# Layer 1's attention rewritten: 32x32 turns on VectorE, value products in four row strips, division on GpSimd

## The chip, the core and the metric

The program runs on one core of a Trainium2 chip. TensorE (PE, with its weight loads shown as PEld) multiplies, VectorE (DVE), ScalarE (ACT) and GpSimd (POOL) do the rest, SyncE (SP) issues most of the DMAs. SBUF and PSUM have 128 partitions[...]. All data is fp32. The metric is the device time of one execution in microseconds.

## The reference

Two layers on x of 8 x 256 x 128 (8 batches of 256 tokens, width 128). Each layer is `x + attention(layernorm(x)) + ffn(layernorm(x))`. Layer 0 has attention with 16 heads of 8 and eight experts of which each token uses two, besides a shared expert. Layer 1, cut to what matters:

```python
q = (x @ Wq + bq)            # 8 heads of 128 a token
k, v = split(x @ Wkv + bkv)  # one key head and one value head of 128
q, k = q + pe, k + pe
scores = (q @ k.T) / sqrt(128)            # causal, inside each batch of 256 tokens
attn = softmax(scores) @ v
out = attn.reshape(2048, 1024) @ Wo
# ffn: one of 8 experts a token (router: softmax, argmax)
h = gelu(x @ w1[e] + b1[e])               # 128 -> 512
y = (h @ w2[e] + b2[e]) * score           # 512 -> 128
```

## The kernel before

The residual stream `acc` stays in SBUF as 16 tiles of 128 tokens; `xT` is the normalised input, turned, with the width on the partitions. Layer 0 fills the first 364 us of the trace: its scores are made in 32-row strips of PE (L768 and L814, two strips each), its experts' tokens come by gathers on POOL (`take`, L464, an indirect DMA for 128 rows), and a small plan (`at_place`) says between which score groups the experts, the way back and layer 1's first layer norms and projections are written. It changes in nothing but what is said under the change.

Layer 1 starts at L1060 with the last of four layer norms, the values (`l1_values`), the router and `routing`, which sorts the tokens into 24 tiles of 128, each with one expert; it is a generator that is moved on a piece at a time. `l1_project` makes q and k of a block of two batches, nine products of 512 columns, each taken out of PSUM by DVE with bias and position added (L701).

The attention of a batch has four steps, by group of four heads (`hg`) and half of the queries (`t`). For t = 0 only 128 keys count, for t = 1 all 256. `l1_probs` multiplies scores into a two-bank PSUM tile, adds the causal mask on DVE (L1090), takes the row maximum (L1092), scales it (L1094), makes four exponentials on ACT with their sums (L1098), and divides on DVE head by head (L1109). `l1_pv`, called for the step before, turns the weights by PE (L1118, a product with the identity for each 128x128 block), copies them out of PSUM on DVE (L1120) and ACT (L1122), multiplies with v (L1125, 512 columns at a time, one PSUM bank tagged `held`), and copies the result to `oT` on ACT (L1128). After the fourth step `l1_finish` multiplies with Wo (L1136) and adds to `acc` (L1144).

Between batches 3 and 4 stand the 24 expert tiles (`l1_group`, six groups of four): a gather of the group's tokens (L466), a turn by PE, four products with w1 (L1039), four Gelus on ACT (L1048), four products with w2 (L1025), bias on DVE (L1032), result to HBM. The weights of a tile (256 + 256 + 64 KB) go through a ring of five, loaded by SP as a tile is done with. Then sixteen gathers fetch every token's result (L1165), and batches 6 and 7 add them to `acc` (L1184).

Nothing here sets an order by hand: the framework schedules the instructions of each engine from the program's order and its own estimates. PSUM is two tiles of two banks for scores (`big`), three single banks (`bank`) and one more (`held`).

Of the kernel before, what the change touches and what calls it, by code (L numbers as in the profile page):

```python
# [10 lines left out]
F32 = mybir.dt.float32  # L11
# [5 lines left out]
P = 128  # L17
# [11 lines left out]
NE = 8  # L29
# [31 lines left out]
def two_layer_kernel(  # L61
# [47 lines left out]

    def ctile(shape, name, pool=const):  # L110
        return pool.tile(shape, F32, tag=name, name=name)
# [82 lines left out]
    pe_s = ctile([P, S], "pe_s")  # L194
    b1_s = ctile([P, NE, NFT], "b1_s")
# [24 lines left out]

    dram = ctx.enter_context(tc.tile_pool(name="dram", bufs=1, space=bass.MemoryType.DRAM))
    xd = [dram.tile([NT, E], F32, name=f"xd{n}") for n in range(2)]
    yg = [dram.tile([n * P, E], F32, name=f"yg{i}") for i, n in enumerate((NS0, NS1))]
# [56 lines left out]
    def layernorm(layer, blk):  # L280
# [4 lines left out]
        for t in range(TPB):  # L285
            nc.vector.bn_stats(st[:, t, :], acc[:, blk * TPB + t, :])
            nc.vector.bn_aggr(mv[:, t, :], st[:, t, :])
        rs = small.tile([P, TPB], F32, tag="ln_rs", name=f"rs_{nm}")
        nc.gpsimd.tensor_scalar_add(rs, mv[:, :, 1], EPS_LN)
        nc.gpsimd.tensor_tensor(rs, rs, minus_half, ALU.pow)  # L290
        off = small.tile([P, TPB], F32, tag="ln_off", name=f"off_{nm}")
        nc.vector.scalar_tensor_tensor(off, mv[:, :, 0], -1.0, rs, ALU.mult, ALU.mult)
        xn = work.tile([P, TPB, E], F32, tag="xn", name=f"xn_{nm}")
        ps = bank(f"lnT_{nm}")
        for t in range(TPB):
            nc.scalar.activation(
                xn[:, t, :],
                acc[:, blk * TPB + t, :],
                AF.Identity,
                bias=off[:, t : t + 1],  # L300
                scale=rs[:, t : t + 1],
            )
            nc.tensor.transpose(ps[:, ts(t, P)], xn[:, t, :], ident)
        nc.scalar.copy(xT[:, ts(blk, BLK)], ps)
# [4 lines left out]
    def softmax8(lg, nm, n):  # L309

        m = small.tile([P, n], F32, tag="r_m", name=f"r_m_{nm}")
        nc.vector.tensor_reduce(m, lg, AX.X, ALU.max)
        d = small.tile([P, n, NE], F32, tag="r_d", name=f"r_d_{nm}", bufs=2)
        nc.vector.tensor_tensor(d, lg, m.unsqueeze(2).to_broadcast([P, n, NE]), ALU.subtract)
        nc.scalar.activation(d, d, AF.Exp)
        s = small.tile([P, n], F32, tag="r_s", name=f"r_s_{nm}")
        nc.vector.tensor_reduce(s, d, AX.X, ALU.add)
        r = small.tile([P, n], F32, tag="r_r", name=f"r_r_{nm}")
        nc.vector.reciprocal(r, s)
        sc = small.tile([P, n, NE], F32, tag="r_sc", name=f"r_sc_{nm}", bufs=2)  # L320
        nc.vector.tensor_tensor(sc, d, r.unsqueeze(2).to_broadcast([P, n, NE]), ALU.mult)
        return sc

    def first_max(sc, nm, n):

        m = small.tile([P, n], F32, tag="f_m", name=f"f_m_{nm}")
        nc.vector.tensor_reduce(m, sc, AX.X, ALU.max)
        key = small.tile([P, n, NE], F32, tag="f_key", name=f"f_key_{nm}", bufs=2)
        nc.vector.tensor_tensor(key, sc, m.unsqueeze(2).to_broadcast([P, n, NE]), ALU.is_equal)
        nc.vector.tensor_tensor(key, key, rev.unsqueeze(1).to_broadcast([P, n, NE]), ALU.mult)  # L330
        k = small.tile([P, n], F32, tag="f_k", name=f"f_k_{nm}")
        nc.vector.tensor_reduce(k, key, AX.X, ALU.max)
        oh = small.tile([P, n, NE], F32, tag="f_oh", name=f"f_oh_{nm}", bufs=2)
        nc.vector.tensor_tensor(oh, key, k.unsqueeze(2).to_broadcast([P, n, NE]), ALU.is_equal)
# [6 lines left out]
    def routing(nm, ohs, n, r):  # L341
# [8 lines left out]
        if len(ohs) > 1:  # L350
            sel = st([P, NTILE, NE], "sel")
            nc.vector.tensor_tensor(sel, ohs[0], ohs[1], ALU.add)
        flat = sel.rearrange("p t e -> p (t e)")
        ps = bank(f"rank_{nm}")
        nc.tensor.matmul(ps[:, :N], lhsT=tri, rhs=flat, start=True, stop=True)
        nc.tensor.matmul(ps[:, ds(N, N)], lhsT=ones, rhs=flat, start=True, stop=True)
        slot = st([P, NTILE, NE], "slot")
        nc.vector.tensor_copy(slot.rearrange("p t e -> p (t e)"), ps[:, :N])
        tot = st([P, NE, NTILE], "tot")
        nc.vector.tensor_copy(tot, ps[:, ds(N, N)].rearrange("p (t e) -> p e t", e=NE))  # L360
        yield
        upto = st([P, NE, NTILE], "upto")
        nc.vector.tensor_tensor_scan(
# [6 lines left out]
        )  # L370
        more = st([P, NE, NTILE], "more")
        nc.vector.tensor_tensor(
# [4 lines left out]
        )  # L377
        yield
        nc.vector.tensor_tensor(tot, upto, tot, ALU.subtract)
        nt = st([P, NE], "nt")  # L380
        nc.vector.tensor_reduce(nt, more, AX.X, ALU.add)
        end = st([P, NE], "end")
        nc.vector.tensor_tensor_scan(end, ones[:, :NE], nt, 0.0, ALU.mult, ALU.add)
        first = st([P, NE], "first")
        nc.vector.tensor_tensor(first, end, nt, ALU.subtract)
        yield
        nc.vector.tensor_tensor(slot, slot, tot.rearrange("p e t -> p t e"), ALU.add)
        nc.vector.scalar_tensor_tensor(
# [6 lines left out]
        )  # L395
        yield
        past = st([P, n, NE], "past")
        nc.vector.tensor_tensor(
# [4 lines left out]
        )  # L403
        r.expert = st([P, n], "ef")
        nc.vector.tensor_reduce(r.expert, past, AX.X, ALU.add)
        nc.vector.tensor_scalar_min(r.expert, r.expert, float(NE - 1))
        r.expert_i = st([P, n], "ei", I32)
        nc.vector.tensor_copy(r.expert_i, r.expert)
# [5 lines left out]
        for k, oh in enumerate(ohs):  # L414
            at = st([P, NTILE, NE], "at")
            nc.vector.tensor_tensor(at, slot, oh, ALU.mult)
            pf = st([P, NTILE], "pf")
            nc.vector.tensor_reduce(pf, at, AX.X, ALU.add)
            pos = st([P, NTILE], f"pos{k}", I32)
            nc.vector.tensor_copy(pos, pf)  # L420
# [3 lines left out]
            nc.vector.tensor_scalar(cut[:, 0, :], pos, 7, None, ALU.arith_shift_right)  # L424
            nc.vector.tensor_scalar(cut[:, 1, :], pos, P - 1, None, ALU.bitwise_and)
            part = st([P, 2, NTILE], "part")
            nc.vector.tensor_copy(part, cut)
            yield
            for q in range(0, NTILE, 4):
                row = work.tile([P, 4, P], F32, tag="ys", name=f"row_{nm}_{k}_{q}")  # L430
                nc.vector.tensor_tensor(
                    row,
                    lane.unsqueeze(1).to_broadcast([P, 4, P]),
                    part[:, 1, ds(q, 4)].unsqueeze(2).to_broadcast([P, 4, P]),
                    ALU.is_equal,
                )
# [312 lines left out]
    for n in range(H1 + 1):  # L749
        at_place(PROJECT1 + n, lambda: next(project1, None))  # L750
# [528 lines left out]
```

## Time and profile before

| what | value |
|---|---|
| runs | 624.95, 628.90, 629.09 us; median 628.9 |
| profiled execution | 657.19 us, span of the trace 655.4 us |
| mean granted clock of TensorE | 0.922 |
| layer 0, 0 to 364 us | PE busy 300.6, DVE 225.8, ACT 131.4, POOL 98.2 us |
| layer 1, 364 to 655.4 us | PE busy 242.2, DVE 167.5, ACT 128.0, POOL 41.5 us |
| end of the output products of batches 0, 1, 2 | 401, 431, 455 us |
| first and last expert product | 479.1 and 543.4 us |
| end of the output products of batches 4, 5, 6, 7 | 577, 604, 628, 652 us |

The trace is of one execution, which took longer than the runs without the profiler. "Busy" is the time in which an engine had an instruction at work; PE's matmuls overlap, so its busy time is more than it needs at full rate. A wait is named by the engine and line that ended it.

### The profile page before, as it was taken

How to read it: one execution, taken by the hardware profiler on the slowest of the kernel's cores; microseconds unless marked ns; L12 is line 12 of the kernel's file. 1: busy time of each engine (PE TensorE's matmuls, PEld its weight loads, DVE VectorE, ACT ScalarE, POOL GpSimd, SP SyncE). 2: the span in 40 equal slices, each digit the busy share in tenths (PEclk: the TensorE clock that was granted, in tenths of full speed). 3: DMA queues.
4: the chain of work that ended last, by engine and by line, in shares of the span. 5: the costliest groups of instructions: out<-in, count | busy, mean ns of one | idle time of the engine just before them, and what ended most of it. 6: DMA issues, size and time to landing. Idle time of an engine off the chain costs nothing.

```text
span 655.4 us, 10882 instructions
## 1 busy us (share of the span) xinstructions
PE 542.7 (83%) x3766; PEld 377.1 (58%) x3766; DVE 393.3 (60%) x961; ACT 259.4 (40%) x686; POOL 139.7 (21%) x177
## 2 busy tenths in 40 slices
PE   2879958989888898768899778989898887689786
PEld 2445636566665674525435556676487786366564
DVE  3688934556667665375685598866762423266753
ACT  0732213354445442131333533243568744132532
POOL 8500052222222204553100000004033204400000
PEclk9985988999999999598799979999898999799889
DMA  8200413234343401110100006001038992100000
GB/s 203 64 3 20 132 33 102 75 99 132 105 112 87 68 18 46 36 49 22 28 17 1 18 0 166 16 1 32 1 112 259 194 264 65 53 9 1 9 9 9
DMA packets 53383, 43.70 MB, mean 67 GB/s; under 512 B 5200, under 2 KB 48272, under 8 KB 53328
## 3 DMA queue, kind: packets, MB, share of 16 engines
q1 hardware_dynamic: 48704, 35.09, 19.1%
q0 software_dynamic: 4048, 7.65, 5.7%
q8 instruction: 30, 0.49, 0.3%
q10 hardware_dynamic: 576, 0.27, 0.2%
q14 instruction: 25, 0.20, 0.1%
HBM read 35.64 MB, written 7.34 MB: 66 GB/s over the span
## 4 chain that ended last, share of the span: by engine, by line
PE 60%; DVE 12%; ACT 11%; issue 7%; POOL 5%; another core or an unknown queue 4%; DMA 1%; SPq 0%; POOLq 0%; ACTq 0%; DVEq 0%
PE s L768 8%; PE o L1125 5%; PE s L1082 5%; PE u L600 5%; PE pv L841 5%; PE wo L1136 4%; PE qk L694 4%; PE s L814 4%; PE d L617 4%; ACT p L1098 3%; PE pT L1118 3%; DVE mx L783 3%; PE qk L512 2%; PE u L1039 2%
## 5 line engine op out<-in xcount | busy, mean ns | idle before, releaser
L466 POOL DMA_INDIRECT xs<-xd,d_ids_l x64 | 64.3, 1004 | 271.5 <-DVE d_ids_l L462 123.8
L826 ACT ACTIVATE eT<-s 128x1024 f32<-128x1024 f32 x64 | 65.3, 1024 | 133.2 <-PE s L814 101.0
L768 PE MATMUL s<-qk 32*128 32x256 f32 x512 | 85.8, 437 | 23.8 <-DVE mx L783 19.1
L783 DVE TENSOR_REDUCE mx<-s 128x4 f32<-128x1024 f32 x64 | 77.5, 1217 | 19.7 <-remote 9.1
L814 PE MATMUL s<-qa,qk 32*128 32x256 f32 x512 | 79.4, 429 | 1.1 <-DVE qa L795 0.7
L768 PEld LDWEIGHTS s<-qk 32*128 32x128 f32 x512 | 48.1, 200 | 50.2 <-DVE mx L783 26.9
L1082 PE MATMUL s<-kT,qT 128*128 128x128 f32 (+1 forms) x256 | 55.7, 355 | 16.8 <-ACT p L1098 16.8
L466 POOL DMA_INDIRECT yt<-yg,d_pos_l x48 | 48.3, 1006 | 90.7 <-DMA yg<-ys 58.7
L1125 PE MATMUL o<-pT,v 128*128 128x512 f32 x96 | 52.8, 662 | 10.9 <-ACT oT L1128 7.2
L1082 PEld LDWEIGHTS s<-kT,qT 128*128 128x128 f32 x256 | 41.3, 203 | 29.8 <-ACT p L1098 23.5
L1098 ACT ACTIVATE p<-s,ms 128x128 f32<-128x128 f32 (+1 forms) x128 | 52.2, 426 | 13.4 <-DVE ms L1094 10.4
L814 PEld LDWEIGHTS s<-qa,qk 32*128 32x128 f32 x512 | 47.1, 199 | 12.3 <-issue 5.6
L1128 ACT COPY oT<-o 128x512 f32<-128x512 f32 x32 | 18.9, 589 | 81.6 <-PE o L1125 71.2
L841 PE MATMUL pv<-eT,va 128*32 128x256 f32 x512 | 43.4, 409 | 1.2 <-ACT eT L826 1.2
L600 PE MATMUL u<-xg,gu_s 128*88 128x128 f32 x320 | 43.0, 278 | 0.6 <-ACT qk L519 0.6
L585 DVE SCALAR_TENSOR_TENSOR sg<-sg,u 88x256 f32<-88x256 f32 x40 | 16.6, 416 | 43.2 <-ACT sg L584 33.2
L617 PE MATMUL d<-dn_s,h 88*128 88x128 f32 x160 | 29.3, 306 | 12.4 <-issue 8.1
L600 PEld LDWEIGHTS u<-xg,gu_s 128*88 128x88 f32 x320 | 38.1, 161 | 1.9 <-ACT qk L519 1.5
L617 PEld LDWEIGHTS d<-dn_s,h 88*128 88x128 f32 x160 | 22.1, 199 | 26.2 <-issue 20.1
L1136 PEld LDWEIGHTS wo<-wo_s,oT 128*128 128x128 f32 x256 | 32.5, 201 | 5.9 <-issue 5.9
L1048 ACT ACTIVATE h<-u,own_b 128x128 f32<-128x128 f32 x96 | 26.6, 378 | 20.6 <-PE u L1039 20.6
L1090 DVE TENSOR_TENSOR s<-s,mask 128x512 f32<-128x512 f32 x32 | 22.2, 694 | 19.7 <-PE s L1082 10.4
(221 smaller groups left out, 937.2 us busy)
## 6 DMA issues: line engine op xcount, KB each, us to landing
w_up<-in_w_dram SPq DMA_DIRECT2D x30, 256.0 KB
gu_s<-in_gu_dram SPq DMA_DIRECT2D x40, 176.0 KB
w_down<-in_w_dram SPq DMA_DIRECT2D x18, 256.0 KB
yg<-ys SPq DMA_DIRECT2D x16, 256.0 KB
dn_s<-in_dn_dram SPq DMA_DIRECT2D x40, 88.0 KB
xd<-xn SPq DMA_DIRECT2D x8, 256.0 KB
bias<-in_b_dram SPq DMA_DIRECT2D x24, 64.0 KB
acc<-in_x_dram SPq DMA_DIRECT2D x4, 256.0 KB
```

The source lines that it names most:

```text
L466: nc.gpsimd.indirect_dma_start(out=dst, out_offset=None, in_=table, in_offset=bass.IndirectOffsetOnAxis(ap=index, axis=0), bounds_check=ta ...
L600: nc.tensor.matmul(ps[:IC, ts(c, P)], lhsT=gu0_s[:, i % RING0, c, :], rhs=xg0.get(i), start=True, stop=True,)
L617: nc.tensor.matmul(ps[:, :P], lhsT=h0[i][:, c, :], rhs=dn0_s[:, i % RING0, c, :], start=(c == 0), stop=(c == 1),)
L768: nc.tensor.matmul(pv[:, jj, t, :], lhsT=qT[r : r + ROW, g, ds(o + t * P, P)], rhs=kT[r : r + ROW, g, ds(o, S)], start=True, stop=True,)
L783: nc.vector.tensor_reduce(m[:, ds(2 * half, 2), :, D0 * ((g + 1) % NG)], pv, AX.X, ALU.max, negate=True)
L814: nc.tensor.matmul(pv[:, jj, c, :], lhsT=kT[r : r + ROW, g, ds(o + c * P, P)], rhs=qa[r : r + ROW, g, :], start=True, stop=True,)
L826: nc.scalar.activation(eT.rearrange("p j c q -> p (j c q)"), ps, AF.Exp, scale=SC0)
L841: nc.tensor.matmul(po[ds(ROW * j, ROW), ts(g % 2, S)], lhsT=va_flat[:, ds(o, ROW)], rhs=eTs[j // 2][:, j % 2, c, :], start=(c == 0), stop= ...
L1082: nc.tensor.matmul(sc[:, hh, :], lhsT=qT[:, 4 * hg + hh, ds(o + t * P, P)], rhs=kT[:, ds(o, nk)], start=True, stop=True,)
L1098: nc.scalar.activation(p[:, hh, :], sc[:, hh, :], AF.Exp, bias=ms[:, hh : hh + 1], scale=SC1, accum_out=sums[:, hh : hh + 1],)
L1125: nc.tensor.matmul(po, lhsT=v1[:, 2 * b + c, :], rhs=pT[:, c, :], start=(c == 0), stop=(c == t))
L1136: nc.tensor.matmul(ps[:, ts(t, P)], lhsT=oT[:, h, ts(t, P)], rhs=wo1_s[:, h, :], start=(h == 0), stop=(h == H1 - 1),)
```

## The change

The diff wraps nearly every instruction of the kernel in `seq(...)`, which from layer 1 on (`ordered[0] = True`) asks the scheduler to keep the order of the program; in layer 0 it does nothing. Beyond that:

- The factor 1/sqrt(128) goes into Wq, its bias and a copy of the positions (`l1_scale`, three operations on POOL), so that the maximum needs no scaling.
- A batch has three parts of 128 x 1024 weights instead of four steps: all heads of t = 0, and two halves of the heads of t = 1.
- The division is one operation a part on POOL (the last part of the last batch on DVE).
- The weights are turned by DVE in 32x32 blocks (`l1_turn`), SBUF to SBUF, without PE. Partition strip n (32 rows) then holds, for every block of 32 keys, the weights of the queries of strip n.
- So v is needed on every strip: `l1_values` writes it to HBM (`vd`), and `l1_spread` reads it back four times, once for each strip, a batch ahead, two buffers.
- `l1_pv` multiplies in four 32-row strips, each into a PSUM bank of its own, over blocks of 32 keys up to the diagonal; it runs one batch late. Four copies (`l1_out`) bring the banks to `oT`.
- Layer norm, values, router, routing, projections, gathers and the adding of results are written into fixed places of the parts (`at1`, `fill`). The last projections are spread over two batches. Fetching the experts' results is written as two gathers a place.
- The expert tiles are written with the first product of a tile before the second of the one before it, in one block, with all exponentials before or after it.
- The end is split: the output of the last batch is made for each half of the queries.

In `routing` a matmul is written one piece after the operations that make its inputs. The diff without the wrapping, cut:

```diff
+    ordered = [False]
+    def seq(ins):
+        return tc.keep_in_program_order(ins) if ordered[0] else ins
...
+    def l1_scale():
+        for dst, src in ((wq1_s, wq1_s), (bq1_s, bq1_s), (peq_s, pe_s)):
+            nc.gpsimd.tensor_scalar_mul(dst, src, SC1)
...
+    at_place(TILES + 10, l1_scale)
...
-    v1 = const.tile([P, NTILE, P], F32, tag="va", name="v1")
+    NQ1 = P // ROW
+    NK1 = S // ROW
+    vrep = const.tile([P, 2, NK1, P], F32, tag="va", name="vrep")
...
+    def l1_spread(b):
+        for n in range(NQ1):
+            nc.sync.dma_start(
+                vrep[ds(ROW * n, ROW), b % 2],
+                vd[ds(b * S, S), :].rearrange("(j k) c -> k j c", k=ROW),
+            )
...
+    def l1_experts():
+        l1_gathered(0)
+        for i in range(NS1 + 1):
+            if i < NS1:
+                l1_up(i)
+            if i % GRP == GRP - 2 and i // GRP + 1 < NS1 // GRP:
+                l1_gathered(i // GRP + 1)
+            if i > 0:
+                l1_down(i - 1)
...
+    PARTS = ((0, 0, H1), (1, 0, H1 // 2), (1, H1 // 2, H1 // 2))
...
-        for hh in range(4):
-            nc.vector.tensor_scalar_mul(p[:, hh, :], p[:, hh, :], rec[:, hh : hh + 1])
+    def l1_weigh(u):
+        rec = small.tile([P, H1], F32, tag="rec1", name=f"rec1_{u.name}")
+        seq(nc.vector.reciprocal(rec[:, : u.nh], u.sums[:, : u.nh]))
+        engine = nc.vector if u.b + 1 == B and u.h0 > 0 else nc.gpsimd
+        seq(engine.tensor_tensor(
+            u.p, u.p, rec[:, : u.nh].unsqueeze(2).to_broadcast([P, u.nh, u.nk]), ALU.mult
+        ))
...
-            for hh in range(4):
-                nc.tensor.transpose(ps[:, ts(hh, P)], p[:, hh, ts(c, P)], ident)
-            if c == 0:
-                nc.vector.tensor_copy(pT[:, c, :], ps)
-            else:
-                nc.scalar.copy(pT[:, c, :], ps)
+    def l1_turn(u):
...
+        seq(nc.vector.transpose(
+            turned[u.b, u.t][:, ds(u.h0, u.nh), :].rearrange("p h k -> p (h k)"),
+            u.p.rearrange("p h k -> p (h k)"),
+        ))
+    def l1_banks(b):
+        return [bank(f"o_{b}_{n}") for n in range(NQ1 - 1)] + [held(f"o_{b}")]
+    def l1_pv(b, t, po):
+        pT = turned[b, t].rearrange("p h (j q) -> p h j q", q=ROW)
+        for j in range(NQ1 * (t + 1)):
+            for n in range(NQ1):
+                end = NQ1 * t + n
+                if j <= end:
+                    r = ROW * n
+                    seq(nc.tensor.matmul(
+                        po[n][:, ts(t, H1 * ROW)],
+                        lhsT=vrep[r : r + ROW, b % 2, j, :],
+                        rhs=pT[r : r + ROW, :, j, :],
+                        start=(j == 0),
+                        stop=(j == end),
+                    ))
...
+    def l1_previous(b):
+        nonlocal oT
+        if b > 0:
+            po = l1_banks(b - 1)
+            for t in range(2):
+                l1_pv(b - 1, t, po)
+            if b + 1 < B:
+                l1_spread(b + 1)
+            oT = work.tile([P, H1, S], F32, tag="c", name=f"oT_{b - 1}")
+            l1_out(slice(None), po, oT)
     for b in range(B):
+        u = [Part(b, k) for k in range(len(PARTS))]
...
+        l1_scores(u[0])
+        if late is not None:
+            l1_turn(late)
+        l1_maxima(u[0])
+        l1_scores(u[1])
+        l1_maxima(u[1])
+        l1_exp(u[0])
+        l1_previous(b)
+        l1_weigh(u[0])
+        fill(b, 0)
         if b == B // 2:
+            l1_exp(u[1])
+            l1_weigh(u[1])
+            l1_turn(u[0])
+            l1_finish(b - 1, (0, 1), oT)
+            l1_experts()
+        l1_scores(u[2])
+        l1_maxima(u[2])
+        if b != B // 2:
+            l1_exp(u[1])
+            l1_turn(u[0])
+        for _ in range(2):
+            next(project1, None)
+        if b != B // 2:
+            l1_weigh(u[1])
+        fill(b, 1)
+        for _ in range(3 - b % 2):
+            next(project1, None)
+        l1_exp(u[2])
...
+        l1_weigh(u[2])
+        l1_turn(u[1])
+        if b > 0 and b != B // 2:
+            l1_finish(b - 1, (0, 1), oT)
+        fill(b, 2)
+        late = u[2]
```

## The prediction

> **What bounds the kernel now.** I read the page's chain of waits first, for where the end is decided. Shares of the span by engine:
>
> ```profile
> PE 60%; DVE 12%; ACT 11%; issue 7%; POOL 5%; another core or an unknown queue 4%; DMA 1%; SPq 0%; POOLq 0%; ACTq 0%; DVEq 0%
> ```
>
> TensorE holds most of it, yet the chain changes engine all the time, so none is full. Then I cut layer 1, which alone is rewritten, into stages by the dates of the output products (L1136), and asked for the busy time of each engine in each. Columns: stage in us, its length, busy us (instructions) of PE, weight loads, DVE, ACT, POOL; granted clock, DMA share, GB/s.
>
> ```profile
> 402.00:432.00 30.00, 27.31 (x131) 18.73 (x130) 21.74 (x50) 10.07 (x38) 0.00 (x0) 0.94 0.26 64
> 432.00:456.00 24.00, 21.17 (x126) 16.36 (x126) 15.67 (x43) 9.93 (x38) 8.15 (x8) 1.00 0.08 20
> 456.00:478.00 22.00, 18.72 (x68) 11.05 (x67) 17.05 (x37) 8.70 (x29) 0.00 (x0) 0.92 0.01 3
> 478.00:544.00 66.00, 58.04 (x450) 54.17 (x449) 23.19 (x62) 47.23 (x132) 16.02 (x16) 0.97 0.78 207
> 551.00:571.00 20.00, 10.64 (x35) 6.17 (x36) 6.83 (x21) 3.70 (x11) 12.71 (x13) 0.83 0.27 72
> 577.00:604.50 27.50, 24.80 (x118) 16.23 (x117) 20.96 (x48) 9.97 (x38) 0.00 (x0) 1.00 0.02 5
> 604.50:628.00 23.50, 20.10 (x105) 15.13 (x105) 15.09 (x39) 9.98 (x38) 0.00 (x0) 0.93 0.02 7
> 628.00:655.40 27.40, 19.02 (x89) 13.46 (x87) 12.53 (x30) 8.57 (x30) 0.00 (x0) 0.88 0.04 10
> ```
>
> Three things are to be seen. A batch without projections takes 23.5 us although PE, which overlaps its own records, needs far less: its full-speed pitch in the timeline is 0.11 us a record of 128 columns (26 records of L1136 in 3.06 us), so scores 5.1, products 5.1, output 3.4 and transposes 2.6 make 16.3 us. The rest is latency between engines. Second, the experts (478 to 544) are held by DMA after a slow start; 3-us stages of the same view, the first two before and the others after it filled:
>
> ```profile
> 479.00:482.00 3.00, 3.00 (x22) 2.84 (x22) 1.50 (x3) 1.77 (x8) 2.29 (x3) 1.00 0.36 96
> 482.00:485.00 3.00, 3.00 (x27) 2.97 (x26) 2.20 (x4) 2.95 (x6) 1.00 (x1) 1.00 0.25 79
> 524.00:527.00 3.00, 2.22 (x20) 1.98 (x20) 1.28 (x3) 0.56 (x3) 0.00 (x0) 1.00 0.91 282
> 527.00:530.00 3.00, 3.00 (x30) 3.00 (x28) 0.29 (x1) 2.18 (x8) 0.00 (x0) 1.00 0.93 271
> ```
>
> From 491 to 539 the mean is 242 GB/s at a share of 0.9 to 1.0. Third, in 551 to 571 sixteen gathers follow each other on POOL, and ACT and DVE stand with no releaser on record:
>
> ```profile
> ACT oT L1128 <- remote: 10.5, 2, 6.5
> PEld o L1125 <- ACT oT L1128: 7.0, 2, 4.8
> DVE pT L1120 <- remote: 5.9, 2, 5.0
> ```
>
> In the chain these "unknown queue" steps are 14.8 us here and 13.0 us at 88 and 269 us, both also bursts of gathers.
>
> **What the Trainium skill says.** *GPSIMD Engine Reference*, 3.1: a two-input tensor_tensor of 2048 fp32 takes 4497 ns. The trace has 1273 ns for 512 (POOL, L896), 2.5 against 2.2 ns an element; they agree roughly. Its section 8 says that GpSimd shares SBUF interfaces with VectorE; no row shows what that costs. *TensorEngine Tiling (Array Packing)*, Key Properties: 32-row tiles load and multiply in parallel, and Gotcha 1 wants different PSUM banks. The trace agrees: sixteen records (8 matmuls of 256 columns, two a strip) need 1.16 us where one matmul takes 0.43:
>
> ```profile
> 355.03 1.16 PE L814 MATMUL s<-qa,qk 32*128 32x256 f32 x16
> ```
>
> *ScalarE: Activation LUTs*, What ACT_TABLE_LOAD costs: 1283 ns for a change of set; the trace has exactly 1283, seven times each at L1048 and L1098.
>
> **The change part by part**, per batch.
> (1) PE. Removed: 24 transposes, 2.6 us. The 6 products of 512 columns (5.1 us) become 36 of 256 columns in strips. Strip 3 has 12 in a row, 12 x 0.43 + 0.2 = 5.4 us (bounds: 5.1, and 15.4 if strips never overlapped). Scores, projections and output stay.
> (2) DVE. Removed: four pT copies of 0.68, 2.7; sixteen divisions, (19.0 + 14.4)/8 = 4.2; four scalings of the maximum, 0.7. Added: three 32x32 turns of 1024. L855 takes 0.71 for 512 and L867 0.44 for 256, so 1.25 each (bounds 1.2 to 1.4), 3.75. Masks and maxima stay within 0.4. DVE falls by some 4 us.
> (3) ACT. pT copies go (1.2); sixteen exponentials and four copies stay. About 8.8 us, beside other work.
> (4) POOL. Three products of 128x1024 by the reciprocal. From L896, 1273/512 x 1024, less one fixed part, 2.45 us; the page's rate gives 2.25. I take 2.4; bounds 2.2 and, if it shares ports badly, 5.
> (5) DMA. Values go to HBM and return fourfold, 512 KB a batch, a batch ahead: at 200 GB/s 2.6 us, hidden behind a batch of 17 us. On SP a spread waits for the strip products that still read its buffer. Behind the spread of batch 2 stand the first five weight tiles (15 DMAs, issued from 396.5 us before, now after batch 1's routing, some 420; used at 485), behind that of batch 5 the sixth tile's, whose own buffer comes free later still, and behind those of batches 6 and 7 output stores that nobody waits for. Nothing charged.
> (6) Start. A scaling of wq1 (POOL, 128x1024, one input, about 1.0) comes ahead of the first layer-norm power at 15.4 us, on which ACT's first xn waits: +1 us. Its load has landed by 16 us, when the DMA rate falls to 26 GB/s. Bounds 0 and 3. The rest of layer 0 is reordered a little; 0 +/- 2, since PE bounds it as before.
> (7) Order. In the built queue of POOL the gathers are not where the source has them: eight (groups 0 and 1) stand ahead of the third product of batch 3, and after the experts ten stand ahead of batch 4's third product, then six ahead of batch 5's first. A gather costs 1.0 + 0.3 us.
>
> **The path of a batch.** From the turn of the last part (0): turn 1.25, strip products from 1.4 to 6.9 on PE, scores of part 3 to 8.6, mask and maximum to 10.6, turn 11.8, reciprocal 12.0, POOL product of part 2 to 14.6, of part 3 to 17.0, next turn. So **17.1 us without projections** against 23.5. Projections put 2 x 0.7 before the reciprocal: 18.6; routing fills DVE, so batches 1 and 2 take 20.4 and 21. Batch 3: product 2 ends at 16.0, eight gathers to 26.4, product 3 to 28.8: 28.9 (PE idle 10 us). Batch 5: 18.6 + 0.8 behind six gathers + 2 for a cold PE clock (0.5 at 497 us) = 21; batch 6 with its combine 17.5.
> Batch 0 with the layer norm now behind POOL's first product, values and router: 363 to 399, before 402.
> Experts: start at batch 4's turn + 15.5. PE alone would need 24 x 1.8 = 43 us, but nineteen tiles of 576 KB, the gathers and the results are 13.5 MB, 56 us at 242 GB/s, and the last tile. Fourteen table loads become two, 15 us of ACT, but what this buys is the slow start alone: 479 to 491 at a mean of 137 GB/s, (242 - 137) x 12 / 242 = 5.2 us. So 59 for the 64.3 between the first and the last expert product (479.1 to 543.4).
> After the experts: result lands 3.4 (543.4 to 546.8 before), ten gathers 13, product 2.4: 19 until the turn. Tail of batch 7, with one product on DVE and the last output split in two: 29.5.
>
> | from | before | after |
> |---|---|---|
> | batch 0 | 39 | 36 |
> | batches 1, 2, 3 | 30, 24, 22 | 20.4, 21, 28.9 |
> | batch 4 with experts | 99 | 15.5 + 59 + 19 = 93.5 |
> | batches 5, 6, 7 | 27.5, 23.5, 27.4 | 21, 17.5, 29.5 |
> | sum | 292.4 | 267.8 |
>
> That is -24.6 of the span of 655.4 (execution 657.2): 632.6. The median of the runs is 628.9, 0.957 of the profiled execution. At that scale the gain is 23.5 us: 605. Whether the stalls of 14.8 us exist in runs without the profiler I can't see; the 28 us between profile and median equal all such stalls. Some of the gain may thus not be there, so I take **608**.
>
> **Rivals.**
> A. *The experts lose their DMA limit*: with ACT out of the way weights stream evenly at the 339 GB/s of one 3-us stage, and PE's 43 us plus fill is the bound, 48. For it: PE at full pitch in 527 to 530. Against: the share of 0.9 to 1.0. 59 - 48 = 11 less: 595.
> B. *The stalls are the profiler's*, or return under the new bursts: 14.8 x 0.957 = 14 us less gain, 620. For it: the 28 us. Against: they sit only on bursts of gathers.
> C. *GpSimd becomes the bound, slower.* About 17 products lie on the path (two a batch, three in batch 0). At 2.4 + 1.45 us each the gain is gone; from 4.3 us the kernel is over 1% slower. At 5 us, DVE and POOL shutting each other out: 17 x 2.6 - 24.6 = +20, 648. For it: shared interfaces. Against: the new DVE work reads one SBUF input.
> D. *The strips don't overlap while they accumulate*: 10 us a batch, 685. Against: the L814 row.
> That the change doesn't do what it says is partly true already: the gathers leave the written order; charged above.
>
> **Chances**: forecast 0.52 (600 to 614), A 0.20, B 0.18, C 0.07, D 0.03. Within 1% (6.3 us, what can be told from none here) is half of B and the edge of C, slower the rest of C and D: faster 0.80, same 0.11, slower 0.09. The range takes in A with POOL at 2.2 and B: 580 to 626.
>
> **What will show it.** Right: groups of 36 strip products near 5.4 us; POOL 128x1024 near 2.4 us; unprojected batch near 17 us; experts near 59 us at a DMA share above 0.9; PE idle 10 us or more before the last turns of batches 3 and 4. Wrong: POOL beyond 4 us; strip products beyond 7; experts under 52, or a batch of 20 and more.

## The result, and the profile after

| | runs | median us | range us | profiled execution us |
|---|---|---|---|---|
| before | 20 | 627.24 | 620.91 to 635.34 | 657.19 (span 655.4) |
| after | 20 | 632.16 | 627.47 to 641.63 | 631.16 (span 629.4) |

After takes 1.0092 of before, 95% interval 1.0064 to 1.0119: 0.9% slower, where 608 us were forecast. Ratios and their intervals leave out runs over 1.5% above the fastest of their kernel; medians and ranges are of all runs.

Yet the profiled executions say the opposite, 26 us less, and after's span of 629.4 is close to the 631 that the forecast's sum gives. That agreement is luck: 10.8 of the 26 us lie in layer 0 (its last addition to `acc` is at 369.5 us in before, at 358.7 in after), where the forecast had no gain at all. The work was to find which of the two, profile or runs, was not what it seemed.

On some occasions of measurement every kernel, before included, took 25 to 40 us longer, and its profile then had engines waiting for an unknown releaser; the first profile of before is of that kind, its timed runs are not. So a time below is given with that of before on the same occasion.

The chain of waits of after, shares of the span by engine; the "unknown queue" of before is gone:

```profile
PE 49%; DVE 21%; issue 7%; POOL 7%; DMA 7%; ACT 5%; SPq 2%; ACTq 0%; POOLq 0%; DVEq 0%
```

Layer 1 of after, cut at its first scores, then at the turn (L1179) of each batch's last part, and at the end. Columns as before: stage in us, its length, busy us of PE, weight loads, DVE, ACT and POOL, granted clock, DMA share, GB/s.

```profile
358.40:392.69 34.29, 24.30 (x124) 18.75 (x122) 20.95 (x53) 9.21 (x38) 6.92 (x5) 0.82 0.29 70
392.69:414.77 22.08, 19.07 (x136) 15.06 (x139) 18.26 (x33) 8.61 (x36) 5.71 (x3) 0.92 0.09 25
414.77:440.15 25.38, 19.06 (x137) 14.20 (x133) 21.08 (x36) 8.61 (x36) 5.68 (x3) 0.93 0.49 139
440.15:470.81 30.66, 26.90 (x204) 21.39 (x202) 21.45 (x33) 8.78 (x36) 14.14 (x11) 0.93 0.14 35
470.81:561.51 90.70, 72.92 (x554) 65.81 (x554) 25.05 (x48) 38.52 (x134) 31.73 (x29) 0.91 0.59 167
561.51:581.80 20.29, 17.73 (x118) 13.78 (x119) 16.04 (x22) 8.62 (x36) 11.75 (x9) 0.82 0.18 46
581.80:598.57 16.77, 16.77 (x158) 14.73 (x158) 15.48 (x20) 8.61 (x36) 5.69 (x3) 1.00 0.18 48
598.57:629.40 30.83, 24.10 (x208) 20.45 (x202) 18.25 (x24) 11.59 (x44) 3.79 (x2) 0.89 0.09 26
```

Against the prediction's column (36, 20.4, 21, 28.9, 93.5, 21, 17.5, 29.5) only batch 2, the third row, is off by more than 3 us. The sum is 271.0 us for 267.8. Layer 1 of after came out as worked out; the gain was lost ahead of it, and in the layer 1 of before that it was measured against.

### The profile page after: what moved, and what is told of

Same layout as the page of the kernel before. It is cut to its first block, busy times and chain, and to the rows that moved or that the text cites. A ratio compares the mean times of both kernels' runs of the same rounds, so it can differ in the third digit from the quotient of the medians.

```text
span 629.4 us, 11372 instructions
## 1 busy us (share of the span) xinstructions
PE 522.2 (83%) x4054; PEld 378.2 (60%) x4054; DVE 382.5 (61%) x771; ACT 233.9 (37%) x662; POOL 187.5 (30%) x203
## 4 chain that ended last, share of the span: by engine, by line
PE 49%; DVE 21%; issue 7%; POOL 7%; DMA 7%; ACT 5%; SPq 2%; ACTq 0%; POOLq 0%; DVEq 0%
PE s L788 8%; PE u L619 5%; PE pv L861 4%; PE d L636 3%; POOL yt L485 3%; PE o L1196 3%; PE s L834 3%; PE s L1134 3%; DVE pT L1179 3%; DMA w_up<-in_w_dram 3%; DVE mx L803 3%; PE wo L1215 2%; PE u L1065 2%; ACT p L1154 2%; PE d L1083 2%
## 5 line engine op out<-in xcount | busy, mean ns | idle before, releaser
L846 ACT ACTIVATE eT<-s 128x1024 f32<-128x1024 f32 x64 | 65.3, 1024 | 117.5 <-PE s L834 117.5
L788 PE MATMUL s<-qk 32*128 32x256 f32 x512 | 88.4, 448 | 15.4 <-DVE mx L803 11.3
L1154 ACT ACTIVATE p<-s,m 128x256 f32<-128x256 f32 (+1 forms) x128 | 52.5, 441 | 108.8 <-DVE m L1148 89.1
L1166 POOL TENSOR_TENSOR p<-p,rec 128x1024 f32<-128x1024 f32 x23 | 43.9, 1910 | 147.8 <-DVE rec L1164 120.5
L834 PE MATMUL s<-qa,qk 32*128 32x256 f32 x512 | 81.6, 439 | 1.0 <-DVE qa L815 0.7
L788 PEld LDWEIGHTS s<-qk 32*128 32x128 f32 x512 | 49.6, 205 | 42.1 <-DVE mx L803 19.8
L1196 PE MATMUL o<-pT,vrep 32*128 32x256 f32 x576 | 52.5, 438 | 13.8 <-DVE pT L1179 12.8
L1196 PEld LDWEIGHTS o<-pT,vrep 32*128 32x128 f32 x576 | 41.7, 215 | 23.5 <-DVE pT L1179 14.7
L1134 PE MATMUL s<-kT,qT 128*128 128x128 f32 (+1 forms) x256 | 49.9, 352 | 3.3 <-ACT p L1154 3.3
L1215 PE MATMUL wo<-wo_s,oT 128*128 128x128 f32 x256 | 34.6, 300 | 5.2 <-DVE qT L720 2.8
L1179 DVE STREAM_TRANSPOSE pT<-p 128x1024 f32<-128x1024 f32 x24 | 29.5, 1228 | 15.5 <-POOL p L1166 15.5
L713 PE MATMUL qk<-xT,wq_s 128*128 128x512 f32 x64 | 33.2, 633 | 6.1 <-DVE qT L720 3.8
```

Source lines behind the costliest of these rows:

```text
L788: seq(nc.tensor.matmul(pv[:, jj, t, :], lhsT=qT[r : r + ROW, g, ds(o + t * P, P)], rhs=kT[r : r + ROW, g, ds(o, S)], start=True, stop=True,))
L834: seq(nc.tensor.matmul(pv[:, jj, c, :], lhsT=kT[r : r + ROW, g, ds(o + c * P, P)], rhs=qa[r : r + ROW, g, :], start=True, stop=True,))
L846: seq(nc.scalar.activation(eT.rearrange("p j c q -> p (j c q)"), ps, AF.Exp, scale=SC0))
L1134: seq(nc.tensor.matmul(u.sc[:, h, :], lhsT=qT[:, u.h0 + h, ds(o + u.t * P, P)], rhs=kT[:, ds(o, u.nk)], start=True, stop=True,))
L1154: seq(nc.scalar.activation(u.p[:, h, :], u.sc[:, h, :], AF.Exp, bias=u.m[:, h : h + 1], accum_out=u.sums[:, h : h + 1],))
L1179: seq(nc.vector.transpose(turned[u.b, u.t][:, ds(u.h0, u.nh), :].rearrange("p h k -> p (h k)"), u.p.rearrange("p h k -> p (h k)"),))
```

## The experiments

**Was the profile of before typical?** The first run is before, unchanged.

> The kernel before, unchanged, profiled once more. Its first profile has a span of 655.4 us, 28 us over the median of its runs (627), and 27.8 us of steps in the chain of waits with no known releaser, all on bursts of gathers. Theory 1, that one execution was an outlier: the new profile has a span of 620 to 633 and less than 5 us of such steps; layer 1 is then some 15 us and layer 0 some 13 us shorter than in the first profile, and the comparison of the two kernels has to be made against this one. Theory 2, the profiler itself brings these stalls to this kernel: span 645 to 660 again, with 10 us or more lost in the result gathers after the experts. Theory 3, a profile and a run agree and the time is lost elsewhere: a span near 627 but with the stalls still there and another part shorter. In theory 1 the granted clock shows too whether TensorE was throttled less than the 0.90 of the changed kernel: if it is 0.92 or more, part of the loss is the clock.

625.55 us (before beside it 624.84), and a profile with a span of 630.2 and no wait for an unknown releaser. Theory 1, though its layer 1 is 7 us shorter and not 15. It is not a typical execution either: 631.93 us, 6.4 over the median of its runs. Its chain of waits, by engine:

```profile
PE 57%; issue 15%; DVE 10%; POOL 7%; ACT 6%; DMA 4%; POOLq 0%; SPq 0%; DVEq 0%
```

The last sum of layer 0, its last addition to `acc`, in this profile and in after's; columns: start, duration, engine, line, operation, tiles, and in brackets the idle time before and its releaser.

```profile
351.26 0.41 DVE L874 TENSOR_TENSOR acc<-wo,acc 128x256 f32<-128x256 f32 x1
```

```profile
358.68 0.42 DVE L894 TENSOR_TENSOR acc<-wo,acc 128x256 f32<-128x256 f32 x1 [1.31 <-PE wo L890]
```

From there to the end before takes 278.9 us (351.3 to 630.2), in its first profile 285.9 (369.5 to 655.4): 7 us less in layer 1, and 18 less in layer 0. With this profile the comparison changes sides: after's layer 0 is 7.4 us longer. Its router starts at 42.9 us for 38.5. The beginning of GpSimd's queue shows why. Before (second profile), then after, and for each the PE product that waits:

```profile
14.80 0.58 POOL L535 TENSOR_TENSOR wg_n<-wg_n,half_power 8x1 f32<-8x1 f32 x1 [2.09 <-DVE wg_n L533]
15.37 2.96 POOL L290 TENSOR_TENSOR rs<-rs,minus_half 128x4 f32<-128x4 f32 x3
...
17.16 1.63 PE L303 MATMUL lnT<-ident,xn 128*128 128x128 f32 x4 [3.11 <-ACT xn L296]
```

```profile
14.46 0.58 POOL L554 TENSOR_TENSOR wg_n<-wg_n,half_power 8x1 f32<-8x1 f32 x1 [1.72 <-DVE wg_n L552]
15.12 2.79 POOL L232 TENSOR_SCALAR wq_s<-wq_s 128x1024 f32<-128x1024 f32 x1
18.00 3.02 POOL L305 TENSOR_TENSOR rs<-rs,minus_half 128x4 f32<-128x4 f32 x3
21.10 0.25 POOL L232 TENSOR_SCALAR bq_s<-bq_s 128x8 f32<-128x8 f32 x1
21.43 0.85 POOL L232 TENSOR_SCALAR peq_s<-pe_s 128x256 f32<-128x256 f32 x1
...
19.83 1.63 PE L318 MATMUL lnT<-ident,xn 128*128 128x128 f32 x4 [6.12 <-ACT xn L311]
```

The scaling takes 2.79 us, not 1.0, and the three powers of the layer norm start 2.6 us late. PE, which waits for them, stands idle for 6.12 us from 13.7 us on, where it stood 3.11 from 14.1.

**The scaling and the gathers, each alone.** Late scaling: the three operations are issued behind the last addition of layer 0 on GpSimd, which has nothing to do then.

```diff
+    scale_after = []
     def l1_scale():
-        for dst, src in ((wq1_s, wq1_s), (bq1_s, bq1_s), (peq_s, pe_s)):
-            nc.gpsimd.tensor_scalar_mul(dst, src, SC1)
+        with tc.issue_after(scale_after[-1]):
+            for dst, src in ((wq1_s, wq1_s), (bq1_s, bq1_s), (peq_s, pe_s)):
+                nc.gpsimd.tensor_scalar_mul(dst, src, SC1)
...
-        seq(nc.gpsimd.tensor_tensor(
+        scale_after.append(nc.gpsimd.tensor_tensor(
             acc[:, ts(blk, TPB), :],
```

> The kernel after, with its three scalings on GpSimd (wq1, bq1 and the positions) issued behind the last of layer 0's additions on that engine, so from about 36 us on, where GpSimd has nothing to do until 90 us; the other queues are the same but for two tiny VectorE operations. Theory 1, the scaling of wq1 at 15.1 us (2.79 us, ahead of the three powers of the layer norm) and the two smaller ones at 21.1 us (1.1 us) are what delays layer 0: in the two profiles the router starts at 42.9 against 38.5 us and the last sum of layer 0 is at 358.7 against 351.3. Then the first power starts at 15.4 us, the router near 38.5, layer 0 ends 4 to 7 us earlier, and the time is 625 to 628 (0.99 of after, equal to before). Theory 2, layer 0 is late for another reason (a lower granted clock, or its changed order): the router still starts near 43 us or the end of layer 0 stays within 2 us of 358, and the time is 630 or more.

The reverse, in before:

```diff
+    def l1_scale():
+        for t in (wq1_s, bq1_s, pe_s):
+            nc.gpsimd.tensor_scalar_mul(t, t, 1.0)
...
+    at_place(TILES + 10, l1_scale)
```

> The kernel before, with the same three GpSimd instructions on the same tiles at the same place in its queue, multiplying by 1.0. Theory 1, they alone delay layer 0: 4 to 7 us slower than before, ratio 1.006 to 1.011, which is the whole difference between the two kernels. Theory 2, the delay of layer 0 has another cause: ratio under 1.004.

Held gathers: in the source each gather of layer 1 stands behind a product, but its mark for the written order doesn't hold an indirect DMA. Here it is queued behind the product by name; the first group of tokens moves from the middle of batch 3 to its end.

```diff
-            take(yt1[n][:, k, :], yg[1], r1.pos[0][:, n + k : n + k + 1])
+            held_take(yt1[n][:, k, :], yg[1], r1.pos[0][:, n + k : n + k + 1])
...
+            with tc.issue_after(next(w for w in reversed(weighed) if w.engine == mybir.EngineType.Pool)):
+                return f(*args)
```

> The kernel after, with the gathers of layer 1 held at their written places: groups 0 and 1 of the tokens behind the third product of batch 3 and the second of batch 4, and each pair of result gathers behind the product that was written before it; only GpSimd's queue changes. Theory 1 (step 7 of the prediction): the products that stand behind gathers are late, by 5.3 us in batch 3 (reciprocal at 463.55, product at 468.87), 9.2 us in batch 4 (550.37, 559.58) and 1 us in batch 5, each of them on the path: 10 to 15 us less, 617 to 622, faster than both kernels. Theory 2, the gathers only move: the experts start later, or the combines on VectorE wait for results that now come late, and PE idles there instead: less than 4 us of gain.

> Both edits together, the late scaling and the held gathers. If both theories 1 hold the gains add, since one lies in the first 40 us and the other behind 455 us: 14 to 22 us less than after, 610 to 618, and faster than before by 1.5 to 2.5 per cent. If the granted clock takes part of it back (0.90 in after against 0.92 in before), the sum falls short of the two single gains by some us with a clock under 0.90.

This was an occasion on which before took 662.05 us. Late scaling 650.81 (0.9757 of before, 0.9647 to 0.9868), held gathers 648.40 (0.9796, 0.9734 to 0.9859), both 642.14 (0.9707, 0.9642 to 0.9772), and **before with the scaling 669.87: 1.0078, 1.0046 to 1.0110**. The last is theory 1 in full: the scaling alone costs 0.8%, some 5 us. What the others gain on after was not to be told, since after wasn't beside them. So they were run again with it:

> The kernel after, unchanged, on the same chip as the three kernels beside it, because before took 625 us on one chip and 662 us on another. Theory 1, the gain in layer 1 of the first pair of profiles was mostly the absence of stalls that only some chips have: on a chip where before takes about 625, after is 0.5 to 1.2 per cent slower (630 to 633); on a chip where before takes about 660, after is 1 to 2 per cent faster (650 to 656), since it has fewer waits behind bursts of gathers. Theory 2, the ratio of the two kernels is the same on all chips: 1.006 to 1.012 on either.

> The late scaling again, now with after beside it. Theory 1 (the scaling delays layer 0, as it did alone in before by 0.8 per cent): 4 to 7 us less than after on the same chip, so 626 where before takes 625, and 645 to 650 where before takes 660. Theory 2 (layer 0 late for another reason): within 2 us of after.

> Late scaling and held gathers, now with after beside them. On the chip of the last runs both edits together were 0.5 per cent under the scaling alone and 0.9 under the gathers alone. Theory 1 (the products that stand behind gathers are late on the path): 9 to 16 us less than after, 616 to 623 where before takes 625. Theory 2 (the gathers only move): no more than the scaling alone.

| where before takes 626.72 | us | of before, 95% interval |
|---|---|---|
| after | 633.42 | 1.0135 (1.0066 to 1.0203) |
| late scaling | 625.61 | 1.0003 (0.9973 to 1.0033) |
| late scaling, held gathers | 610.42 | 0.9783 (0.9715 to 0.9852) |
| products on VectorE (below) | 620.71 | 0.9879 (0.9845 to 0.9913) |

The scaling costs after 7.8 us (633.42 to 625.61), more than the 2.6 us by which it delays the layer norm. After's second profile shows where more of it comes from, in windows with the columns of the stages above, granted clock, DMA share and GB/s last:

```profile
20.00:30.00 10.00, 7.41 (x28) 3.62 (x27) 4.89 (x12) 7.70 (x18) 7.07 (x9) 0.98 0.28 80
30.00:40.00 10.00, 9.73 (x45) 6.00 (x44) 5.24 (x7) 4.02 (x12) 1.27 (x1) 0.50 0.10 28
```

and the kernel with late scaling:

```profile
20.00:30.00 10.00, 9.01 (x52) 5.29 (x52) 6.99 (x10) 7.57 (x20) 3.40 (x3) 1.00 0.19 54
30.00:40.00 10.00, 7.68 (x68) 5.11 (x60) 7.21 (x14) 3.96 (x14) 5.14 (x4) 1.00 0.10 29
```

From 30 us on PE gets half its clock, and needs 9.73 us for 45 products where the other makes 68 in 7.68. The router starts at 47.2 us here, 49.6 in before with the scaling, 38.0 with late scaling. All five profiles with the early scaling have the long gap of PE (5.99 to 6.12 us) and a clock of 0.50 from 30 to 32 us; the fifteen without it have a gap of 3.1 us and a clock of 1.00 from 20 to 40 us. So it is shown that the early scaling brings the half clock. That the length of the gap does, is not shown. *TensorE: Matmul & The Clock Gate* in the Trainium skill, HAM oscillation, says that gaps of PE above some 3.4 us bring half the clock. Here the clock stayed at 1.00 for 9 us behind the gap of 6.12, and fell at the end of a second, shorter one:

```profile
29.13 1.14 PE L516 MATMUL vg<-wvg_s,xT 128*128 128x137 f32 x4 [1.35 <-DVE qk L534]
```

This is after's first profile, with a clock of 1.00 until 29.0 us and 0.50 from 29.5 on. The same wait takes 0.69 us in the second profile of before and 0.27 with late scaling. The page's limit is therefore not confirmed by these traces.

The gathers cost 15.2 us more (625.61 to 610.42, both with late scaling). GpSimd's queue in after, around the third products of batches 3 and 4, whose reciprocals start at 463.55 and 550.37 us:

```profile
466.55 1.00 POOL L485 DMA_INDIRECT xs<-xd,d_ids_l  x1 [0.30 <-issue]
467.85 1.00 POOL L485 DMA_INDIRECT xs<-xd,d_ids_l  x1 [0.30 <-issue]
468.87 1.91 POOL L1166 TENSOR_TENSOR p<-p,rec 128x1024 f32<-128x1024 f32 x1
...
558.55 1.00 POOL L485 DMA_INDIRECT yt<-yg,d_pos_l  x1 [0.30 <-issue]
559.58 1.91 POOL L1166 TENSOR_TENSOR p<-p,rec 128x1024 f32<-128x1024 f32 x1
```

The products start 5.3 and 9.2 us behind them, one in batch 5 another 1.0: 15.5 us, close to what holding the gathers gave in the runs (in one pair of profiles, from the last sum of layer 0 to the end, it gave 12.9, 271.0 to 258.1). With the gathers held the second product waits for its reciprocal instead:

```profile
529.62 1.00 POOL L485 DMA_INDIRECT yt<-yg,d_pos_l  x1 [0.30 <-issue]
532.21 1.89 POOL L1166 TENSOR_TENSOR p<-p,rec 128x1024 f32<-128x1024 f32 x1 [1.59 <-DVE rec L1164]
```

**The division's place.** `engine = nc.vector` for every product of after, nothing else.

> The kernel after with the products by the reciprocal on VectorE instead of GpSimd, in the same place of its order; TensorE's order is unchanged. Theory 1, GpSimd as the place of the products costs more than it saves: seven VectorE instructions of after that start beside a product take 1.6 to 2.1 us instead of 0.2 to 0.4 and end with it (10 us in all), each product adds a hop between engines, and in batches 3 to 5 products stand behind gathers (15 us): on VectorE a product takes about 1.2 us, twenty-three of them 28 us of VectorE, of which batches with slack hide half: 5 to 15 us less than after. Theory 2, VectorE becomes the bound (15 to 16 us busy of 17 in a batch without projections, plus 3.6): 5 to 20 us more than after.

12.7 us less than after (633.42 to 620.71), inside the range of theory 1. Its layer 1 takes 260.5 us from the last sum of layer 0, after's 269.8. Products on VectorE take 1.22 us and can't stand behind gathers, which by themselves account for 15.2 us above; so this run alone doesn't show that the engine matters. The other half of the theory, that GpSimd's products hold up VectorE, is to be seen in after, DVE first and GpSimd's product below it:

```profile
429.60 1.90 DVE L442 CAST d_part_l<-d_cut_l 128x32 f32<-128x32 int32 x1
429.57 1.89 POOL L1166 TENSOR_TENSOR p<-p,rec 128x1024 f32<-128x1024 f32 x1 [5.89 <-DVE d_cut_l L440]
```

The same cast took 0.17 us in layer 0, with no product beside it. Whether that is on the path was asked of a mixture: late scaling, held gathers, and VectorE for the products of batches 2, 5 and 6 (`if u.b in (2, 5, 6)`).

> The kernel after with the late scaling and the held gathers, a third time, as the measure for the three kernels beside it, which are all built from it. It took 610.4 us where before took 626.7 (0.978), and 642 where before took 662 (0.971): 0.97 to 0.98 again.

> Late scaling and held gathers, and the products by the reciprocal of batches 2, 5 and 6 on VectorE. In the profiles of the two pure versions batch 2 took 25.4 us with GpSimd and 23.6 with VectorE, batches 5 and 6 together 40.3 and 36.3, the tail 28.5 and 30.6. Theory 1, GpSimd's product holds up the VectorE instructions that start beside it: 4 to 7 us less than late and held alone, 603 to 607 where before takes 626. Theory 2, these differences come from the gathers that stood in other places in the two kernels: within 2 us.

Neither: 653.25 us against 646.38 (before 663.80). Batch 2 took 25.0 us for 25.3, so its excess is not from there; batch 6 gained 1.8 us, but batch 5 took 31.3 for 20.1, with one wait of VectorE for an unknown releaser of 12.3 us. With no products on GpSimd between them the gathers of batch 5 follow each other again (574 to 591 us), and the long wait comes with them, so the mixture tests two things at once. That products on GpSimd cost time on the path is not shown; what batch 2 has too much is open.

**The rest of layer 0.** In before the first scores of layer 1 stand among the last products of layer 0; in after the written order puts them behind. PE in before (second profile), then in after, around the last product of layer 0 (`wo<-wo_s,aT`):

```profile
345.00 0.94 PE L1082 MATMUL s<-kT,qT 128*128 128x128 f32 x6
...
346.85 2.22 PE L1082 MATMUL s<-kT,qT 128*128 128x128 f32 x10
350.28 0.71 PE L870 MATMUL wo<-wo_s,aT 128*128 128x128 f32 x4 [1.21 <-DVE aT L867]
```

```profile
357.42 1.22 PE L890 MATMUL wo<-wo_s,aT 128*128 128x128 f32 x4 [1.91 <-DVE aT L887]
358.44 2.78 PE L1134 MATMUL s<-kT,qT 128*128 128x128 f32 x15
```

Two edits on top of late scaling and held gathers. One binds the order only after the first exponentials of batch 0:

```diff
-    ordered[0] = True
...
         l1_exp(u[0])
+        ordered[0] = True
         l1_previous(b)
```

> Late scaling and held gathers, and the first scores and maxima of layer 1 not bound to the written order, so that TensorE issues the first of them between the last products of layer 0. In the profile of before the first scores start 6.3 us ahead of layer 0's last sum (345.0 and 351.3), in after 0.3 us ahead of it (358.4 and 358.7). Theory 1, this lost overlap is part of what layer 0 lost: 2 to 5 us less than late and held alone. Theory 2, TensorE fills the time with other work of layer 0 anyway or batch 0 then waits for its layer norm: within 2 us.

The other puts the token lists' products of layer 0's routing back into the step of their rows, which makes PE's queue in layer 0 that of before:

```diff
-            for q in range(0, NTILE + 4, 4):
+            lag = 0 if nm == "l0" else 4
+            for q in range(0, NTILE + lag, 4):
...
-                if q > 0:
+                if lag == 0:
+                    made = (row, col)
+                if q > 0 if lag else q < NTILE:
```

> Late scaling and held gathers, and in layer 0's routing the products of the token lists in the same step as their rows, as in before, so that TensorE's queue in layer 0 is that of before, instruction by instruction. Theory 1, the shift by a step delays the lists and with them the first gather: in the runs the first 100 us of after stay 4 to 8 us longer than those of before even with the late scaling (worked out from the medians: layers behind the first gather take the same 260 us in every profile), so 4 to 7 us less than late and held alone. Theory 2, the shift doesn't matter (the first gather is at 84.0 to 92.2 us in four profiles with the late scaling, at 83.5 and 91.3 in two of before): within 2 us.

638.77 and 642.51 us, beside 646.38 for late and held alone, four runs each. In the profiles the open start shortens the time from the last sum of layer 0 to the end from 267.0 to 262.5 us. Again, with both edits together, where before took 624.61:

> Late scaling, held gathers and unbound first scores again, with the measure of before in more runs. On another chip it was 7.6 us under late and held alone (638.8 and 646.4, before 663.8). Theory 1 (the overlap with layer 0's end is regained): where before takes about 626, 604 to 608, 0.965 to 0.972 of before; where before takes about 662, 637 to 641. Theory 2 (the 7.6 us were the spread of four runs): 0.974 to 0.980 again.

> The same with the token lists' products of layer 0 in the order of before. On another chip that order alone was 3.9 us under late and held, with ranges that overlap (638.9 to 642.8 and 641.6 to 649.1). Theory 1 (the shift by one step costs 4 to 8 us in layer 0): 3 to 7 us under the kernel beside it. Theory 2 (it costs nothing): within 2 us.

613.28 (0.9849 of before, 0.9802 to 0.9896) and **605.53 (0.9699, 0.9653 to 0.9744)**. The open start did not repeat its gain over late and held (0.9783 on another occasion, with an overlapping interval), although the time behind the last sum is again 3 us shorter (255.0 for 258.1); what it is worth in the runs is not settled. The lists' order gave 7.8 us, with ranges that don't overlap (601.9 to 609.2, 610.9 to 619.5). Then each side of it by itself, the shift in before and both edits of layer 0 taken back in after:

> The kernel before with one part of the change alone: in layer 0's routing the products of the token lists come one step after their rows. TensorE's queue in layer 0 is then that of after, instruction by instruction; layer 1 is that of before. Theory 1, the shift costs 4 to 8 us in layer 0 (without it the version with late scaling and held gathers was 7.8 us shorter): 1.006 to 1.013 of before. Theory 2, it costs nothing by itself, and the 7.8 us were owed to something else that the shift did there: within 0.4 per cent of before.

> The kernel after with both changes to layer 0 taken back: the scaling behind the last of layer 0's additions on GpSimd, and the token lists' products in the step of their rows. TensorE's queue in layer 0 is that of before; layer 1 is that of after, gathers ahead of the products included. Theory 1, layer 1's own gain is what the profiles show from the last sum of layer 0 to the end, 278.9 us in before and 270.7, 269.8 and 271.0 in three profiles with after's layer 1, 8 us: 0.983 to 0.990 of before, and all of the loss of 0.9 per cent lies in layer 0's two changes. Theory 2, layer 1 gains nothing in runs: 0.995 or more.

> The kernel after with both changes to layer 0 taken back, once more, since before took 660 us beside it the last time and its waits behind gathers weigh differently there. If before takes about 625 now: theory 1 (layer 1's own gain of some 8 us is real in runs, and the loss lies in layer 0's two changes), 0.983 to 0.992 of before, so 614 to 620; theory 2 (layer 1 gains nothing in runs, or the shift of the lists costs nothing), 0.996 to 1.003, as with the late scaling alone (1.0003). If before takes about 660 again: 0.974 to 0.987 as before, which tells neither.

Before took 659.74 and 664.30 on these occasions. The shift in before: 1.0040, 0.9991 to 1.0089, no clear answer. Layer 0 undone: 0.9801 (0.9736 to 0.9866) and 0.9793 (0.9746 to 0.9840), no more than late scaling alone on such an occasion (0.9757). What the shift costs by itself is therefore not settled: 7.8 us in one pair, 3.9 with overlapping ranges in the other, no clear answer elsewhere.

A rival was left untested: TensorE's clock. The expectation of the second profile of before names it (0.92 or more there would make part of the loss the clock), and that profile has 0.921 where after's first has 0.900. On the occasion of the table after's four runs have a mean granted clock of 0.889 to 0.897, before's 0.921 to 0.948, late scaling still 0.896 to 0.909. Before's own runs, in its second measurement, go from 621.2 us at 0.945 to 631.9 at 0.921. Part of this lies in the first 100 us, where the stretches at half clock differ from one execution to the next: two kernels with the same layer 0 (late scaling, without and with held gathers) reach its last sum at 353.9 and 344.9 us. So a date in layer 0 from one profile is uncertain by some 9 us, and only the runs can carry a price there. Whether the changes lower the clock or a lower clock hides their gain was not separated.

## Why the prediction was wrong, by its own steps

Forecast was -20.9 us (608 for 628.9), measured +5.8 (0.92% of 627): a miss of 26.7.

- **Step (6), the start, failed first.** It priced the scaling of wq1 at "about 1.0" and the delay at +1, 0 to 3, and the sum of the table leaves even this +1 out. The operation takes 2.79 us, and in all five profiles with it PE ran at half clock from 30 to 32 us at least, with 1.00 in the others, which the step did not ask about. Shown both ways in the runs: 1.0078 when added to before (some 5 us), 7.8 us when moved in after.
- **Step (6), "the rest of layer 0, 0 +/- 2", failed too.** It looked at layer 0's own order alone. The written order took away that layer 1's first scores ran inside layer 0's end: 6.3 us ahead of its last sum in before, 0.3 in after. That is 6 us by the dates of the two profiles; setting it free gave back 4.5 and 3.1 us of profile behind the last sum, and no settled amount in the runs, so the price is argued, not shown.
- **The scaling to the runs, and rival B.** The ratio 0.957 spread the 28 us between profile and runs evenly. They weren't even: 7.0 us lay in layer 1 (285.9 and 278.9 from the last sum) and were counted as gain. The 3 us between 605 and 608 allowed for less than half of it. Rival B saw that the stalls might not be in the runs, but took them for the profiler's: the second profile of before has none.
- **Layer 1, steps (1) to (4), held.** Strip groups 5.4 to 5.5 us at full clock for 5.4, turns 1.23 for 1.25, the batch without projections 16.8 for 17.1, experts 57 (486.1 to 543.0) for 59 at a DMA share of 0.86 in place of 0.9, so rival A's 48 did not come. The product of 128x1024 took 1.91 us for 2.4, under its lower bound of 2.2. Batch 2 is 4.4 us over, the sum 3.2.
- **Step (7), the hoisted gathers, held in kind.** It charged 8, 10 and 6 gathers ahead of the products. They stood there, but the third products of batches 3 and 4 were late by 5.3 and 9.2 us, not by the 10 and 13 of a whole row of gathers, and PE's idle time before the turns was 3.75 and 7.70 us where 10 or more was named as a sign.
- **Step (5)** charged nothing for the spread, and nothing is seen of it: batch 3's spread lands at 431.5 us and is first read at 466.3. The chain of waits names it at 428.8 us for 2.7 us, but what VectorE did there was the cast shown above, which ended at the same time.

All signs that the prediction named lie in layer 1, and most of them came; none looked at layer 0, where it failed.

In the terms of the profiles the sum closes. The forecast was -24.6 us, and the second profile of before and that of after differ by -0.8 (630.2, 629.4). The 23.8 between are 13.4 by which the first scores start later (345.0 to 358.4: 7.4 of layer 0's last sum and 6.0 of lost overlap), 7.2 by which layer 1 of before is shorter, counted from its first scores (292.4 to 285.2), and 3.2 by which that of after is longer. The step to the runs does not close: they say +5.8. Most of these 6.6 us is that before's second profile is of an execution 6.4 over the median of its runs, so no trace shows where they lie. The shifted lists, which gave 7.8 in one pair, and the clock are candidates, not more.

Of the rivals, C named GpSimd but with the wrong mechanism: a product under 3.85 us was not to decide, and at 1.91 it didn't. The queue around it did, by the scaling at the start and by the gathers.

## What to carry to other kernels

Before a gain is read from a profile, its execution must be one like the runs: compare its time with their range, and where it lies outside, price no stage from it. One profile inside the range can still be 6 us from the median, and the same layer 0 ended 9 us apart in two. An operation that is added "beside" the work goes where the built queue puts it: look up what waits behind it there, and compare TensorE's granted clock behind that place too: here a delay of 2.6 us cost 7.8. Check on the built queue that a written order holds for the DMAs too; gathers ahead of short work on GpSimd cost 15 us here, more than the 8 us by which layer 1 is shorter in the profiles (278.9 to 270.7).

## What the runs showed of the hardware that was not expected

- On GpSimd a one-input `tensor_scalar` of 128x1024 took 2.79 us and a two-input `tensor_tensor` of the same size 1.91.
- VectorE instructions that start while a GpSimd product runs are of two kinds. Those with two SBUF inputs, and casts, ended with the product or up to 0.3 us behind it, after 0.9 to 2.1 us where 0.2 to 0.5 are usual; turns of 128x1024 (1.21 us beside, 1.23 alone) and operations that read PSUM were not longer. *GPSIMD Engine Reference* in the Trainium skill, section 1, Specifications, names two SBUF inputs and two-port modes as contending for the shared interface. For two SBUF inputs the trace agrees; the price here was up to the whole product.
- The granted clock stood at 0.50 for stretches of up to 30 us in which PE was busy 99% of the time (52 to 82 us in the second profile of before; 50 to 63 in its first). Within one kernel the time goes with the mean clock, as the figures of before's runs above show.
- The waits for an unknown releaser are 29 to 60 us, added over ACT and DVE, in the twelve profiles of the longer occasions and none in the eight others; one and the same chip had both, with before at 662.1 and at 624.6 us. What causes them was not found.
